# A two-layer transformer kernel: first norm by tile, two early norms by transfers, the last unit's exponentials next to its projections, the last tile by column halves

## The chip, the cores and the metric

The kernel runs on one core of a Trainium2 chip. Times are device microseconds of one launch. Three runs of the kernel before gave 637.04, 637.12 and 637.52; the median is 637.12. The profile is of one more execution, which took 638.02.

## The reference

Four sublayers, each wrapped the same way: `x = x + layernorm(f(layernorm(x)))`, on x of 2 batches x 512 rows x 256 columns, all in float32.

```python
x = x + _layernorm(_L0_attn_ref(_layernorm(x), ...))   # its own norm with gain and bias, q, k, v of 16 heads of 128,
                                                       # rope on q and k, causal softmax, out projection, residual
x = x + _layernorm(_L0_ffn_ref(_layernorm(x), ...))    # 256 -> 2048 gate and up (4-bit weights with block scales),
                                                       # gelu(gate) * up, 2048 -> 256
x = x + _layernorm(_L1_attn_ref(_layernorm(x), ...))   # linear attention, below
x = x + _layernorm(_L1_ffn_ref(_layernorm(x), ...))    # 256 -> 688 gate and up, weights lut[idx], silu(gate) * up, 688 -> 256

def _L1_attn_ref(x, W_qkv, W_out):
    q, k, v = jnp.split(x @ W_qkv.T, 3, axis=-1)       # 16 heads of 16
    q, k = phi(q), phi(k)                              # elu(x) + 1
    kv_cumsum = jnp.cumsum(k * v, axis=2)
    k_cumsum = jnp.cumsum(k, axis=2)
    out = q * kv_cumsum / (q * k_cumsum + EPS)
    return out @ W_out.T * HD ** (-0.5)
```

## The kernel before

The 1024 rows are 8 tiles of 128 rows; two tiles are a unit, so a batch has two units and there are four (u = 0 to 3). x stays on chip from its load to its last store.

**Order of the work.** Each engine runs its own list of instructions in order; the lists are written by hand. PE's list is the backbone: `slot(i)` for the 32 heads of both batches (scores of head i, the projections of q and k for head i+1, the out projection of head i-2, attention over values of head i-1), then `ffn_hidden` and `ffn_out` of the four units, then `silu_hidden` and `silu_out` of the four units. The work between the stages (norms, linear attention, stores) is written as generators, "chains", that yield when they would have to wait. `now` is a planner's clock of PE, `times` holds planned ends of all instructions, `until(tile)` is how long a tile still takes by that plan, and `poll()`, called between pieces of PE work, goes on with each chain that is due. So a chain's instructions stand in the engines' lists where the plan says that their inputs will be ready. Plan and chip may differ: then an engine waits.

**Loads.** `load(name, gg)` issues a weight group's transfer on SP's queue; a group serves two heads, and each weight has two buffers. At the start, SP and ACT issue the four tiles of batch 0 in turn, then ACT issues `cols_sb` (biases, gain and bias of the norm), SP the weights. `load("q", 2)` and `load("k", 2)` stand in slot 1 ahead of `turned_p(1)`. `turned_p(i)` turns the softmax of head i in 32x32 blocks on DVE and moves the blocks to their place by four transfers (pT; one buffer); head 0's are issued by SP and ACT, the others by SP.

**First norm** (`first_norms(0, 0.0)`). While x lands, PE runs 12 matmuls of the identity as warm-ups (`warm_up(WARM)`). DVE takes the statistics of the tiles (bn_stats, bn_aggr, then ve), POOL raises ve to -0.5 (rstd), DVE works out shift = -mean * rstd for tiles 0 and 1, and ACT applies n = x * rstd + shift; tiles 2 and 3 are centred and scaled on DVE. PE transposes n in order of tiles into two PSUM banks, with one more warm-up behind tile 0, and gain and bias are applied on the way out of PSUM: by ACT for the half of tiles 0 and 1, by DVE for that of 2 and 3. The first projection, of q for head 0, is done in the same two halves.

**Norms between the stages** (`norms(u, y, stage, to)`). The statistics of y (POOL works out ve, rstd and shift), a wait for all of them, then for each tile x += y * rstd on DVE and the statistics of the new x; then ACT writes the normed x to n, and n is transposed into `to`. Two ways of doing that: with `by_blocks`, two DVE transposes of 32x32 blocks and four SP transfers put it in place; otherwise four PE transposes into one PSUM bank and two ACT copies, each copy written behind the two transposes of its half. Before, `by_blocks` holds only when `late` has its pools, that is after attention, and never for the last norm (u = 3, stage 3). So the norms of units 0 and 1 of stage 1, which run beside the attention of batch 1, are transposed on PE.

**Linear attention** (`linear_attention(u)`). Projections of k, q and v (8 matmul records of 128x256 each on PE); ACT takes relu(-k), relu(k) and the same of q, with a yield after each; after v's projection ACT takes exp of the two negative parts, then DVE adds -1 and 1 and POOL adds the parts. Running sums on DVE (ks, kvs), the quotient (den), and the output projection into a bank with tag "o". `silu_out` and `ffn_out` use the banks of tag "o" too; each tag has two banks.

**End.** `silu_out(u)` gives for each of two tiles six matmuls (12 records) into a bank "o", and begins `written`: statistics, rstd and shift on POOL, x += y * rstd, x += shift on DVE, one SP transfer of 128 KB.

Of the kernel before, what the change touches and what calls it, by code (L numbers as in the profile page):

```python
# [32 lines left out]
HT = 2  # L33
# [7 lines left out]
NEG = -1e30  # L41
WARM = 12
REST = INTER - (NO - 1) * P
# [145 lines left out]
def sandwich_kernel(  # L189
# [96 lines left out]

    x0 = [const.tile([P, NT, D], F32, name=f"x0_{b}") for b in range(B)]
    for t in range(NT):
        (scalar if t % 2 else sync).dma_start(
            out=x0[0][:, t, :], in_=x[0][t * P : (t + 1) * P, :]  # L290
        )
    cols_sb = const.tile([P, 3 * NH + 2 * NK], F32, name="cols_sb")
    scalar.dma_start(out=cols_sb, in_=cols)
    cos_sb = const.tile([P, S], F32, name="cos_sb")
# [47 lines left out]
    def norms(u, y, stage, to, eps=EPS, strided=False):  # L342
# [4 lines left out]
        first = [stats(t, eps) for t in y]  # L347
        yield until(*(t for f in first for t in f))
        second = []
        for j in range(HT):  # L350
            add_scaled(x[j], y[j], first[j][0])
            second.append(stats(x[j], EPS))
# [3 lines left out]

        by_blocks = late and (u, stage) != (NUNIT - 1, 3)
        for j in range(HT):
# [24 lines left out]
        else:  # L383
            pt = bank("t")
            for kc in range(NK):
                for j in range(HT):
                    transpose(
                        pt[:, kc * TU + j * P : kc * TU + (j + 1) * P],
                        n[:, j, kc * P : (kc + 1) * P],
                    )  # L390
                scalar.copy(
                    to[:, :, kc].rearrange("p a j t -> p j a t"),
                    pt[:, kc * TU : (kc + 1) * TU].rearrange("p (j a t) -> p j a t", j=HT, a=4),
                )
# [103 lines left out]
    with ExitStack() as at:  # L498
# [54 lines left out]
        def first_norms(b, wait):  # L553
# [19 lines left out]
            def shifted(k, ts):  # L573
                vector.scalar_tensor_tensor(
                    shift[:, k, ts], mv[:, ts, 0], -1.0, rstd[:, k, ts], ALU.mult, ALU.mult
                )

            def norm(k, t, to):
                scalar.activation(
                    to,  # L580
                    x0[b][:, t, :],
                    AF.Identity,
                    bias=shift[:, k, t : t + 1],
                    scale=rstd[:, k, t : t + 1],
                )

            def finished(t):
                shifted(0, slice(t, t + 1))
                norm(0, t, n[t // HT][:, t % HT, :])
# [46 lines left out]
            else:  # L636


                statistics(0)
                variance(0)  # L640
                statistics(1)
                factor(0)
                variance(1)
                statistics(2)
                factor(1)
                variance(2)
                statistics(3)
                factor(2)
                variance(3)
                finished(0)  # L650
                factor(3)
                finished(1)
                centred(2)
# [8 lines left out]
                for j in range(2):  # L662
                    for kc in range(NK):
                        affine(
                            vector if j else scalar,
                            xT0[b][:, kc, j * TU : (j + 1) * TU],
                            halves[j][:, kc * TU : (kc + 1) * TU],
                            kc,
                        )
# [321 lines left out]
        def slot(i):  # L991
            b, h = divmod(i, NH)
            g2, odd = divmod(i, HG)
            if odd == 0:
                load("v", g2 + 2)
# [72 lines left out]
            if i == 0:  # L1068
                values(1, 0)
            elif i == 1:  # L1070
                load("q", 2)
                load("k", 2)
            if now_in:
# [47 lines left out]
    def linear_attention(u):  # L1121
# [18 lines left out]

        k, q, v, ek, eq = of("k"), of("q"), of("v"), of("ek"), of("eq")
        for part, e, f in ((1, ek, k), (0, eq, q)):
            ps = project(part, "mm")
            scalar.activation(flat(e), ps, AF.Relu, scale=-1.0)
            scalar.activation(flat(f), ps, AF.Relu)
            yield until(f)
        ps = project(2, "s")
        scalar.copy(flat(v), ps)

        for e, f in ((ek, k), (eq, q)):  # L1150
            scalar.activation(e, e, AF.Exp, scale=-1.0)
        yield until(ek, eq)
        for e, f in ((ek, k), (eq, q)):
            vector.tensor_scalar(e, e, -1.0, 1.0, ALU.add, ALU.add)
            pool.tensor_add(f, f, e)
        yield until(k, v)
# [10 lines left out]
        running_sum(ks, k)  # L1167
        yield until(ks, q)
        vector.tensor_mul(den, q, ks)
# [12 lines left out]
        yield until(lT)  # L1182
        po = bank("o")
        for t in range(HT):
# [59 lines left out]
    def silu_out(u):  # L1244
        for t in range(HT):
            po = bank("o")[:, :D]
            for o in range(NO):
                matmul(po, hT2[u % 2][:, o, t * P : (t + 1) * P], wd[:, o, :], o == 0, o == NO - 1)
                if o % 2 and o + 1 < NO:
                    yield  # L1250
            begin(written(u, t, po))
            yield

    def written(u, j, y):
        x = xs[u][:, j, :]
        rstd, shift = stats(y, EPS)
        yield until(rstd, shift)
        add_scaled(x, y, rstd)
        vector.tensor_scalar(x, x, shift, None, ALU.add)
        row = ((u % 2) * HT + j) * P  # L1260
        sync.dma_start(out=out[u // 2][row : row + P], in_=x)

# [105 lines left out]
```

## Time and profile before

| | |
|---|---|
| median of 3 runs | 637.12 us (637.04 to 637.52) |
| the profiled execution | 638.02 us, span of its instructions 636.2 us |
| busy share of the span | PE 98%, DVE 77%, ACT 47%, POOL 43% |
| granted TensorE clock | 0.999 |
| first projection starts | 8.18 us |
| heads 2 to 30, one slot each | 11.20 us in most |
| last matmul ends, x of the last tile is done | 630.8, 633.4 us |

Time is counted in us from the span's start. A row of the timeline has the start, the duration (of merged rows, from the first start to the last end), the engine, the line, the operation, the tile written and those read, the shapes and the number of instructions; in brackets is the idle time of the engine just before, and what ended it. Line 181 and line 272 are helpers that record every operation of DVE, ACT and POOL, and every matmul: the tiles tell which one it is. A float32 matmul has two records. PEld is PE's loading of weights; SPq and ACTq are rows of an instruction queue that issues transfers. Ends of matmuls are modelled, so consecutive rows of PE overlap by some 0.2 us, and PE's time is better counted from start to start.

### The profile page before, as it was taken

How to read it: one execution, taken by the hardware profiler on the slowest of the kernel's cores; microseconds unless marked ns; L12 is line 12 of the kernel's file. 1: busy time of each engine (PE TensorE's matmuls, PEld its weight loads, DVE VectorE, ACT ScalarE, POOL GpSimd, SP SyncE). 2: the span in 40 equal slices, each digit the busy share in tenths (PEclk: the TensorE clock that was granted, in tenths of full speed). 3: DMA queues.
4: the chain of work that ended last, by engine and by line, in shares of the span. 5: the costliest groups of instructions: out<-in, count | busy, mean ns of one | idle time of the engine just before them, and what ended most of it. 6: DMA issues, size and time to landing. Idle time of an engine off the chain costs nothing.

```text
span 636.2 us, 8205 instructions
## 1 busy us (share of the span) xinstructions
PE 622.6 (98%) x2506; PEld 463.1 (73%) x2506; DVE 487.8 (77%) x1152; ACT 299.6 (47%) x656; POOL 275.1 (43%) x350
## 2 busy tenths in 40 slices
PE   8999999999999999999999999999999999999896
PEld 6566666666666666665666688888888888888775
DVE  7869889877887989898988999769966651662852
ACT  3645666656655556666565651232233223333220
POOL 3354657445454465754767400450350350351441
PEclk9999999999999999999999999999999999999999
DMA  7456475564556547446352421311000000001010
GB/s 249 117 142 182 119 180 148 112 183 122 141 150 160 164 117 189 129 109 186 87 139 73 100 61 45 108 28 31 2 18 16 1 17 18 0 20 32 0 35 16
DMA packets 41276, 59.54 MB, mean 94 GB/s; under 512 B 4880, under 2 KB 28688, under 8 KB 41232
## 3 DMA queue, kind: packets, MB, share of 16 engines
q1 hardware_dynamic: 40512, 58.30, 34.8%
q10 hardware_dynamic: 720, 0.72, 0.5%
q8 instruction: 20, 0.33, 0.2%
q14 instruction: 24, 0.20, 0.1%
HBM read 28.33 MB, written 1.05 MB: 46 GB/s over the span
## 4 chain that ended last, share of the span: by engine, by line
PE 91%; DVE 4%; ACT 1%; DMA 1%; issue 1%; POOL 1%; ACTq 0%; POOLq 0%; DVEq 0%
PE ps_mm L272 37%; PE ps_s L272 20%; PE ps_o L272 20%; PE ps_t L272 13%; DMA pT<-turned 1%; PE ps_o L535 1%; DVE rr L181 1%; DVE den L181 1%; PE ps_t L278 0%; DVE x L181 0%; DVE st L181 0%; ACT L181 0%; DVE ra L181 0%; DVE ks L181 0%; POOL rstd L181 0%
## 5 line engine op out<-in xcount | busy, mean ns | idle before, releaser
L181 POOL TENSOR_TENSOR wg<-wg,scratch 128x752 f32<-128x752 f32 x30 | 53.5, 1784 | 98.7 <-DVE scratch L181 98.7
L181 DVE SCALAR_TENSOR_TENSOR rr<-ps_mm,cols_sb,sin_sb 64x512 f32<-64x512 f32 (+1 forms) x126 | 93.4, 741 | 2.6 <-ACT ra L181 0.2
L272 PE MATMUL ps_mm<-xT,wg 128*128 128x256 f32 (+1 forms) x352 | 85.4, 380 | 0.8 <-ACT si L181 0.7
L181 ACT ACTIVATE p<-p,mn 128x512 f32<-128x512 f32 (+3 forms) x128 | 70.6, 553 | 30.4 <-DVE mn L181 30.4
L272 PE MATMUL ps_s<-xT,wu 128*128 128x256 f32 x336 | 81.0, 379 | 0.0
L272 PE MATMUL ps_o<-wd,hT 128*128 128x256 f32 x352 | 78.2, 379 | 0.4 <-DVE x L181 0.4
L272 PE MATMUL ps_t<-pT,v 128*128 128x512 f32 (+3 forms) x256 | 74.3, 433 | 1.9 <-DMA pT<-turned 1.9
L272 PEld LDWEIGHTS ps_o<-wd,hT 128*128 128x128 f32 x352 | 66.8, 190 | 9.8 <-DVE x L181 0.8
L272 PEld LDWEIGHTS ps_mm<-xT,wg 128*128 128x128 f32 (+1 forms) x352 | 66.1, 189 | 10.7 <-ACT si L181 1.1
L181 DVE CUSTOM_DVE_ANT_0 p<-ps_s,mask 128x512 f32<-128x512 f32 (+2 forms) x96 | 46.0, 510 | 32.0 <-PE ps_s L272 31.6
L272 PEld LDWEIGHTS ps_s<-xT,wu 128*128 128x128 f32 x336 | 63.8, 190 | 8.7
L272 PEld LDWEIGHTS ps_t<-pT,v 128*128 128x128 f32 x256 | 48.6, 190 | 29.3 <-issue 15.3
L181 ACT ACTIVATE p<-p,rs 128x512 f32<-128x512 f32 (+3 forms) x128 | 61.4, 550 | 11.2 <-DVE rs L181 9.2
L272 PEld LDWEIGHTS ps_o<-wo,oT 128*128 128x128 f32 x256 | 48.6, 190 | 19.0 <-issue 13.6
L181 POOL TENSOR_TENSOR qT<-ra,rr 128x512 f32<-128x512 f32 x32 | 40.8, 1276 | 48.4 <-DVE rr L181 46.3
L272 PE MATMUL ps_s<-kT,qT 128*128 128x512 f32 (+2 forms) x192 | 60.8, 452 | 0.2 <-DVE kT L181 0.2
L272 PE MATMUL ps_o<-wo,oT 128*128 128x256 f32 x256 | 60.5, 379 | 0.0
L272 PE MATMUL ps_mm<-xT,wq 128*128 128x512 f32 (+1 forms) x128 | 58.4, 580 | 0.2 <-ACT xT L181 0.2
L272 PE MATMUL ps_mm<-xT,wk 128*128 128x512 f32 x124 | 58.3, 592 | 0.0
L181 DVE STREAM_TRANSPOSE turned<-p 128x512 f32<-128x512 f32 (+3 forms) x128 | 54.1, 481 | 2.1 <-DMA pT<-turned 1.0
L272 PEld LDWEIGHTS ps_s<-kT,qT 128*128 128x128 f32 x192 | 36.0, 190 | 26.8 <-issue 16.0
L272 PE MATMUL ps_mm<-wv,xTv 128*128 128x256 f32 x232 | 54.9, 379 | 0.0
(129 smaller groups left out, 917.0 us busy)
## 6 DMA issues: line engine op xcount, KB each, us to landing
pT<-turned SPq DMA_DIRECT2D x126, 208.0 KB, 3.8
wo<-in_wo SPq DMA_DIRECT2D x17, 256.0 KB, 4.0
wq<-in_wq SPq DMA_DIRECT2D x16, 256.0 KB, 3.9
wk<-in_wk SPq DMA_DIRECT2D x16, 256.0 KB, 4.0
wv<-in_wv SPq DMA_DIRECT2D x16, 256.0 KB, 4.1
xT<-tr SPq DMA_DIRECT2D x36, 64.0 KB, 2.2
pk_g<-in_gate_p SPq DMA_DIRECT2D x4, 256.0 KB, 5.2
sc_g<-in_gate_s SPq DMA_DIRECT2D x8, 128.0 KB, 4.4
```

The costliest lines, as they stand in the source:

```text
L181: return write(*args, **more)
L272: nc.tensor.matmul(out, lhsT=lhsT, rhs=rhs, start=start, stop=stop, **more)
L535: nc.tensor.matmul(warm[:, :P], lhsT=ident, rhs=ident, start=True, stop=True)
```

## The change

- First norm: `cols_sb` is loaded ahead of x; SP loads tiles 0 and 1, ACT tiles 2 and 3. Statistics, variance and factor are written tile by tile; the shift of tiles 0 and 1 is worked out on POOL; ACT applies gain and bias to all four quarters. There are 9 warm-ups instead of 12.
- The loads of q's and k's group 2 move from slot 1, ahead of `turned_p(1)`, to the start of slot 2, behind it.
- `norms` waits for each tile's rstd alone, and `by_blocks` holds for all norms but the last one. In the last one, both copies stand behind all four transposes.
- For the last unit, `linear_attention` writes exp, the DVE addition and POOL's addition right behind each projection, without the yields between; its output goes to a bank of tag "t".
- The last tile of `silu_out` is computed by two column halves of 128. Its `written` takes statistics by half, works out ve on DVE, centres y on DVE, adds it scaled to x in one step, and stores 64 rows each through SP and ACT.

```diff
-WARM = 12
+WARM = 9
...
+    cols_sb = const.tile([P, 3 * NH + 2 * NK], F32, name="cols_sb")
+    scalar.dma_start(out=cols_sb, in_=cols)
     for t in range(NT):
-        (scalar if t % 2 else sync).dma_start(
+        (scalar if t >= HT else sync).dma_start(
             out=x0[0][:, t, :], in_=x[0][t * P : (t + 1) * P, :]
         )
-    cols_sb = const.tile([P, 3 * NH + 2 * NK], F32, name="cols_sb")
-    scalar.dma_start(out=cols_sb, in_=cols)
...
         first = [stats(t, eps) for t in y]
-        yield until(*(t for f in first for t in f))
         second = []
         for j in range(HT):
+            yield until(first[j][0])
             add_scaled(x[j], y[j], first[j][0])
             second.append(stats(x[j], EPS))
...
-        by_blocks = late and (u, stage) != (NUNIT - 1, 3)
+        by_blocks = (u, stage) != (NUNIT - 1, 3)
...
+            for kc in range(NK):
                 scalar.copy(
                     to[:, :, kc].rearrange("p a j t -> p j a t"),
...
+            def shifted_row(t):
+                pool.tensor_scalar(
+                    shift[:, 0, t : t + 1], mv[:, t, 0:1], rstd[:, 0, t : t + 1], -1.0, ALU.mult, ALU.mult
+                )
...
-            def finished(t):
-                shifted(0, slice(t, t + 1))
+            def finished(t, engine=vector):
+                if engine is pool:
+                    shifted_row(t)
+                else:
+                    shifted(0, slice(t, t + 1))
                 norm(0, t, n[t // HT][:, t % HT, :])
...
-                statistics(0)
-                variance(0)
-                statistics(1)
-                factor(0)
-                variance(1)
-                statistics(2)
-                factor(1)
-                variance(2)
-                statistics(3)
-                factor(2)
-                variance(3)
-                finished(0)
-                factor(3)
-                finished(1)
+                for t in range(NT):
+                    statistics(t)
+                    variance(t)
+                    factor(t)
+                    if t < HT:
+                        finished(t, pool)
                 centred(2)
                 centred(3)
...
                         affine(
-                            vector if j else scalar,
+                            scalar,
...
         def slot(i):
             b, h = divmod(i, NH)
             g2, odd = divmod(i, HG)
+            if i == 2:
+                load("q", 2)
+                load("k", 2)
...
-            elif i == 1:
-                load("q", 2)
-                load("k", 2)
             if now_in:
                 turned_p(i)
...
+        last = u == NUNIT - 1
         for part, e, f in ((1, ek, k), (0, eq, q)):
             ps = project(part, "mm")
             scalar.activation(flat(e), ps, AF.Relu, scale=-1.0)
             scalar.activation(flat(f), ps, AF.Relu)
-            yield until(f)
+            if last:
+                scalar.activation(e, e, AF.Exp, scale=-1.0)
+                vector.tensor_scalar(e, e, -1.0, 1.0, ALU.add, ALU.add)
+                pool.tensor_add(f, f, e)
+            else:
+                yield until(f)
         ps = project(2, "s")
         scalar.copy(flat(v), ps)
...
         running_sum(ks, k)
-        yield until(ks, q)
+        if not last:
+            yield until(ks, q)
...
-        po = bank("o")
+        po = bank("t" if last else "o")
...
+            last = (u, t) == (NUNIT - 1, HT - 1)
+            for cs in [slice(0, P), slice(P, D)] if last else [slice(0, D)]:
+                for o in range(NO):
+                    matmul(
+                        po[:, cs],
+                        hT2[u % 2][:, o, t * P : (t + 1) * P],
+                        wd[:, o, cs],
+                        o == 0,
+                        o == NO - 1,
+                    )
...
+        st = small.tile([P, 2, 6], F32, tag="st", name="st_last")
+        mv = small.tile([P, 2], F32, tag="mv", name="mv_last")
+        for c in range(2):
+            vector.bn_stats(st[:, c, :], y[:, c * P : (c + 1) * P])
+        vector.bn_aggr(mv, st)
+        ve = small.tile([P, 1], F32, tag="ve", name="ve_last")
+        vector.tensor_scalar(ve, mv[:, 1:2], EPS, None, ALU.add)
+        rstd = small.tile([P, 1], F32, tag="rstd", name="rstd_last")
+        pool.tensor_tensor(rstd, ve, mhalf[:, :1], ALU.pow)
+        centred = acts.tile([P, HT, D], F32, tag="ln", name="centred")[:, 0, :]
+        vector.tensor_scalar(centred, y, mv[:, 0:1], None, ALU.subtract)
+        add_scaled(x, centred, rstd)
+        for engine, rows in ((sync, slice(0, P // 2)), (scalar, slice(P // 2, P))):
+            engine.dma_start(out=to[rows], in_=x[rows])
```

## The prediction

> **What bounds the kernel now.** I read the page first, then PE's waits, then the timelines around them.
>
> ```profile
> PE 622.6 (98%) x2506; PEld 463.1 (73%) x2506; DVE 487.8 (77%) x1152; ACT 299.6 (47%) x656; POOL 275.1 (43%) x350
> PE 91%; DVE 4%; ACT 1%; DMA 1%; issue 1%; POOL 1%; ACTq 0%; POOLq 0%; DVEq 0%
> ```
>
> The first line is busy time by engine, the second the chain that ended last, both of the page. PE's own waits (total, times, longest):
>
> ```profile
> PE ps_t L272 <- DMA pT<-turned: 1.9, 1, 1.9
> PE ps_o L272 <- DVE x L181: 1.5, 2, 1.1
> ```
>
> PE is the path: only what PE does not have to do, or its few waits, can shorten the span, plus the two ends where it has no work. The largest stand here, in its timeline (start, length; the bracket is the idle time before; two more, 0.36 at 611.44 and 0.82 at 294.14, are of the same kinds):
>
> ```profile
> 32.35 2.39 PE L272 MATMUL ps_t<-pT,v 128*128 128x512 f32 x8 [1.90 <-DMA pT<-turned]
> ...
> 255.70 2.32 PE L272 MATMUL ps_t<-pT,v 128*128 128x512 f32 x8
> 257.85 0.38 PE L278 MATMUL ps_t<-ident,ln 128*128 128x128 f32 x2
> 259.06 0.44 PE L278 MATMUL ps_t<-ident,ln 128*128 128x128 f32 x2 [0.82 <-ACT xT L181]
> 259.33 1.89 PE L272 MATMUL ps_mm<-wv,xTv 128*128 128x256 f32 x8
> ...
> 590.41 1.13 PE L272 MATMUL ps_mm<-xT,wg 128*128 128x256 f32 x4 [0.73 <-ACT si L181]
> ...
> 603.91 1.99 PE L272 MATMUL ps_o<-wout_sb,lT 128*128 128x256 f32 x8 [1.15 <-DVE x L181]
> ...
> 614.58 0.33 PE L278 MATMUL ps_t<-ident,ln 128*128 128x128 f32 x1 [0.17 <-ACT ln L181]
> 615.37 0.44 PE L278 MATMUL ps_t<-ident,ln 128*128 128x128 f32 x2 [0.46 <-ACT xT L181]
> ```
>
> Ends of matmuls are modelled, so I count by starts: a 128x256 record takes 0.216 us (8 in 1.73 from 259.33 to 261.06), a 128x128 one 0.11.
>
> **The first norm.** The first useful matmul (ps_mm<-xT,wq) starts at 8.18.
>
> ```profile
> 1.38 5.49 PE L535 MATMUL ps_o<-ident 128*128 128x128 f32 x24 [1.38 <-POOL ident masks.py:199]
> 6.66 0.43 PE L278 MATMUL ps_t<-ident,n 128*128 128x128 f32 x2
> ...
> 4.12 2.11 POOL L181 TENSOR_TENSOR rstd<-ve,mhalf 128x1 f32<-128x1 f32 x4 [2.32 <-DVE ve L181]
> 5.34 1.09 ACT L181 ACTIVATE n<-x,shift,rstd 128x256 f32<-128x256 f32 x2 [1.71 <-DVE shift L181]
> ```
>
> ACT has tile 0's n at 5.94, but its transposes stand behind 12 warm-ups until 6.66. With 9 (24 records in 5.28 by starts, so 0.44 a warm-up) they end at 5.4. New chain: statistics of tile 0 at 3.03 + 0.43, aggregate 0.18, ve 0.14 and gaps: rstd starts at 3.92 instead of 4.12. On POOL follow in order rstd 0 (0.55), shift 0 (0.27, as a later norm's at 629.94), rstd 1, shift 1, rstd 2, rstd 3, about 0.08 between: shift 1 at 5.8, rstd 3 at 6.9 (before: last rstd at 6.23). So ACT's second n ends at 6.4 as before, and DVE's centred tile 3 comes at 7.4 instead of 6.68. Transposes run in order, tile 3's last; q's first matmul then starts at about 7.65, 0.53 earlier, and its second half, with the affine now on ACT (4 x 0.51 from 6.8, ending 8.85 against DVE's 9.00), ends 0.65 earlier. ACT hides these two affines; DVE, idle from 6.7 to 8.0, loses nothing else. The queues keep their three ACT issues; cols_sb moving ahead of x costs x little (26 KB against 128 KB a tile) and may land tile 0 0.25 earlier, as it now shares the engines with less. Bounds without the clock: 0 (POOL's chain) to 0.9; I take **-0.65**, nearest the rows.
>
> Against it stands the clock. In the rows, warm-up records are 0.213 apart up to 6.45 and 0.11 apart from 6.8: half rate for 5.3 us of PE work. "TensorE: Matmul & The Clock Gate" of the Trainium skill, Part 1, says that the rate doubles after one busy window of about 3.4 us of a free-running clock, and Part 4 that transposes don't count as busy. By the rule, 12 warm-ups contain a whole window in (5.3 - 3.4)/3.4, 55% of phases, 9 (4.0 us) in 17%; else the first surely full window starts with the projections, and half rate until 11.1 to 14.5 costs half of 3.4 to 6.8 us, 1.7 to 3.4. The row would give -0.65, the rule up to +2.8. I take the row's: the 9 warm-ups, the one between transposes and the projections fill about three quarters of the window that opened at 3.3 here, and I doubt that a window must be wholly full. The range keeps the other end.
>
> **q2, k2 loads behind turned_p(1).** Before, SP issues wq and wk at 26.03 and 27.50, while head 0's pT (24.68 to 26.90 on SP and ACT) is in flight; ACT's two take a median 6.2 us to land against 3.8 on the page. Behind head 1's pT they no longer share its engines. PE is due at 28.56 + 1.73 = 30.29 and starts at 32.35: 2.06 lost. What is late next is kT of head 2: POOL ends it at 32.12 + 1.27 = 33.39, and its scores stand at 34.59, so 1.2 less a hop of 0.14 can be gained. **-1.05** (0.5 to 1.1). The price: SP now issues wq, wk at about 38, ahead of wv, wo and the pk_g load, which move back some 1.5 us each; pk_g has until ACT's cast at 46.47, and head 4's projection is at 48. Head 1's pT keeps its place ahead of them, head 2's (issued from 44.56) may land up to 1.5 later out of 2.3 spare. Hidden; without that cover some 0.5.
>
> **Two early norms by transfers** (units 0 and 1, stage 1). From 255.70 to 259.33 is 3.63, where a slot without a norm takes 2.16: 1.47 of PE each, twice **2.94** (four transposes and a wait for ACT's copy, at 257.85 and 292.94). New: two DVE transposes per norm (0.44 each in later norms), four SP issues of 0.6; ACT drops two copies of 0.37. SP waits for tr, but behind it stand loads, and the next pT, which comes later on DVE anyway; xT1 is needed 60 us later. DVE is what pays, since the slot also gets shorter:
>
> ```profile
> core 0: us, PE busy (x) PEld busy (x) DVE busy (x) ACT busy (x) POOL busy (x), PEclk, DMA share, GB/s
> 237.12:248.33 11.21, 11.21 (x42) 7.15 (x40) 10.97 (x27) 7.02 (x17) 8.63 (x10) 1.00 0.63 170
> 248.33:261.06 12.73, 11.91 (x46) 7.75 (x45) 11.67 (x32) 8.66 (x21) 7.08 (x7) 1.00 0.50 120
> 261.06:272.26 11.20, 11.20 (x41) 7.29 (x40) 9.21 (x21) 6.20 (x15) 6.62 (x7) 1.00 0.55 159
> ```
>
> 11.67 + 0.88 = 12.55 in a slot of 11.25: DVE falls 1.3 behind, and the next slot has 1.99 free. The second norm: 11.22 + 0.88 in 11.2, 0.9 behind, then 1.43 free. kT has only 0.4 to 0.8 to spare before PE's scores, so I charge 0.45 (0 to 2.2): **-2.5**.
>
> **The last unit.** ACT does k's and q's Exp at 587.30, after two yields; now they follow each projection. Three projections run in one piece, 576.57 to 581.75 (24 x 0.216), putting back silu_out(0)'s rest and hidden(1), which are not late. ACT: relus 578.49 to 579.58, table 1.28, Exp to 581.5, q's relus and Exp to 583.3, v 583.9, table again 585.2; the next si is due at about 586.3, so the 0.73 wait goes, and still two table loads. k is ready at 583.3 instead of 592.87; DVE and POOL then need 11.0 as before (592.91 to 603.91): lT at 595, xT3 by 607. PE has hidden(1), hidden(2), silu_out(1), silu_out(2) and wout until 613, so it does not wait for them. The "t" bank takes away the wait for written's x at 603.91 and at 611.44; all transposes ahead of the copies, and a cover of silu_out(2), the waits from 614.58. By starts from 588.65 to 616.81: 0.9, 1.3 and 0.5 at those three, 0.3 + 0.7 + 0.4 around the transposes, 0.3 of slow first records: 4.4. I leave 0.5 for transposes that still meet ACT: **-3.9** (2.5 to 4.4). The first[j][0] waits shorten chains that PE doesn't wait for: nothing; their cover is PE's backlog.
>
> **The last tile.**
>
> ```profile
> 631.56 0.22 POOL L181 TENSOR_SCALAR ve<-mv 128x1 f32<-128x1 f32 x1 [1.36 <-DVE mv L181]
> 633.06 0.35 DVE L181 TENSOR_SCALAR x<-x,shift 128x256 f32<-128x256 f32 x1
> ```
>
> Before, the chain is bn_stats at 630.82, aggregate, POOL's ve and pow, two DVE steps on x. From PE's end (630.79) to x is 2.62. New: second half's statistics about 0.30, aggregate 0.22, ve on DVE 0.17, pow 0.65, x 0.52, and 0.17 because DVE is in the first tile's x until PE ends: 2.03, so 0.6 less. Centring (0.45) hides under pow. 24 records of 0.112 instead of 12 of 0.216 cost PE 0.1; half a transfer on each of two queues, 0 to 0.2 less of 1.7. **-0.55** (0.2 to 0.8).
>
> **Sum** 0.65 + 1.05 + 2.5 + 3.9 + 0.55 = 8.65. The profiled execution took 638.02 (span 636.2, 1.8 around it), 0.9 above the median of 637.12; off the median: **628.5**.
>
> **Rivals.**
> - The clock slips one window at the start: 1.7 more, 630.2. For it the skill's rule, against it the nearly full window.
> - DVE becomes the bound of the norm slots and stays behind into the next ones: the full 2.2, perhaps more: 630.5 to 632. For it DVE's 10.97 of 11.21 in the slot before the first norm; against, the free slots after each.
> - The planner, whose times order the queues, sets the last unit's steps elsewhere and PE waits again: 3 of the 3.9 are not gained, 631.5.
> - Slower than before: PE stays at half rate. Each us of it costs 0.5: the gains are eaten when it lasts 17 us past 7.7, and from 20 us (27.7) on the kernel is over 0.2% slower; 30 us of it give 643.5. For it only the same page's note that the gate has been seen stuck for over 50 us; against, PE is busy from 8 on but for 2 us.
>
> **How the numbers follow.** A measurement here tells 0.2% (1.3 us) from no change. As computed 0.60 (626.8 to 629.8), clock slip 0.15, DVE 0.11, planner 0.07, slower or near nothing 0.07. Range 626.6 to 632.3: it leaves out the last case and the ends. Faster 0.92, same 0.03, slower 0.05.
>
> **What would show it.** Right: no L278 rows on ln at 250 to 300; ps_t<-pT first at about 30.6; no idle bracket over 0.3 on PE after 586; k's scan near 584; first wq matmul near 7.6 and 0.216 apart. Wrong: wq records 0.43 apart (clock); waits of PE on kT or on DVE p at 260 to 310; PE waits in 590 to 616; a POOL shift ending after 6.

## The result, and the profile after

Four runs of the changed kernel gave 631.17, 631.60, 632.86 and 633.01: median 632.23 us, against 637.32 (637.04 to 638.08) for the kernel before on the same chip. The ratio is 0.9917, with a 95% interval of 0.9897 to 0.9937. It is faster, by 5.1 us where 8.65 were predicted. The profiled execution took 631.60, its span is 629.8; before it was 636.2, so the two traces differ by 6.4.

The page's busy times and its chain that ended last:

```profile
PE 619.6 (98%) x2504; PEld 461.7 (73%) x2504; DVE 487.7 (77%) x1154; ACT 298.2 (47%) x654; POOL 277.8 (44%) x350
PE 95%; DMA 2%; DVE 1%; issue 0%; ACT 0%; POOL 0%; ACTq 0%; POOLq 0%
```

PE has 3.0 us less work (eight transposes and six warm-up records are gone, 12 records came with the halves of the last tile) and 95% of the chain instead of 91%. PE's waits (total, times, longest):

```profile
PE ps_t L272 <- DMA pT<-turned: 1.5, 1, 1.5
...
PE ps_t L278 <- DVE n L181: 1.3, 2, 0.9
PE ps_t L278 <- ACT ln L181: 0.4, 1, 0.4
```

The waits for x in the last stage, 1.5 before, are gone; a wait for `n`, in the first norm, is new. PE's timeline at the places that the prediction showed:

```profile
7.77 0.44 PE L278 MATMUL ps_t<-ident,n 128*128 128x128 f32 x2 [0.90 <-DVE n L181]
8.62 0.44 PE L278 MATMUL ps_t<-ident,n 128*128 128x128 f32 x2 [0.41 <-DVE n L181]
8.89 1.97 PE L272 MATMUL ps_mm<-xT,wq 128*128 128x256 f32 x8
...
16.13 1.96 PE L272 MATMUL ps_s<-kT,qT 128*128 128x512 f32 x6
...
32.54 2.39 PE L272 MATMUL ps_t<-pT,v 128*128 128x512 f32 x8 [1.49 <-DMA pT<-turned]
...
255.91 2.32 PE L272 MATMUL ps_t<-pT,v 128*128 128x512 f32 x8
258.07 1.89 PE L272 MATMUL ps_mm<-wv,xTv 128*128 128x256 f32 x8
...
304.61 1.89 PE L272 MATMUL ps_s<-kT,qT 128*128 128x512 f32 x6
...
594.55 1.89 PE L272 MATMUL ps_t<-wout_sb,lT 128*128 128x256 f32 x8
...
605.53 0.55 PE L278 MATMUL ps_t<-ident,ln 128*128 128x128 f32 x3 [0.35 <-ACT ln L181]
...
618.87 5.43 PE L272 MATMUL ps_o<-wd,hT 128*128 128x256 f32 x36
```

Read the rows as stretches between places that both traces have. In the trace of before, those that the prediction does not show are:

```profile
15.53 1.96 PE L272 MATMUL ps_s<-kT,qT 128*128 128x512 f32 x6 [0.17 <-DVE kT L181]
...
307.35 1.89 PE L272 MATMUL ps_s<-kT,qT 128*128 128x512 f32 x6
...
625.44 5.34 PE L272 MATMUL ps_o<-wd,hT 128*128 128x256 f32 x24
```

| stretch, to the start of | before | after | this stretch gave | predicted |
|---|---|---|---|---|
| scores of head 0 | 15.53 | 16.13 | +0.59 | -0.65 |
| values of head 0 (pT) | 32.36 | 32.54 | -0.41 | -1.05 |
| scores of head 26, past both norms | 307.35 | 304.61 | -2.92 | -2.5 |
| last `silu_out` | 625.44 | 618.87 | -3.83 | -3.9 |
| end of the span | 636.2 | 629.8 | +0.19 | -0.55 |

(The column "this stretch gave" is the change in how long the stretch lasts, by unrounded starts.) The two large steps came as worked out. The start and the end, worked out as gains, are losses in this pair of traces, and head 0's pT gives less than half.

Not all rows are equally firm. In this trace and those of the experiments below, the third stretch lasts 272.04 to 272.15 us in twelve of the thirteen traces that have the norms by transfers (the other, with a piece at half clock, 273.47), against 274.99 before. The fourth lasts 314.25 to 314.27 in all ten that keep the last unit as changed, against 318.09 and 318.12 in the two with the old one. The first two rows have no such firmness: the kernel with only the norms changed has the same code as the kernel before up to there, and its trace reached scores of head 0 at 15.24 instead of 15.53, and values of head 0 at 31.36 instead of 32.36.

Where the start goes is told by the timeline of DVE and ACT's queue:

```profile
1.17 0.93 ACTq L163 DMA_DIRECT2D x<-in_x  x2
...
5.18 0.15 DVE L181 TENSOR_SCALAR ve<-mv 128x1 f32<-128x1 f32 x1
6.56 0.43 DVE L181 BATCH_NORM_STATS2 st<-x 128x6 f32<-128x256 f32 x1 [1.22 <-DMA x<-in_x]
...
8.15 0.41 DVE L181 TENSOR_SCALAR n<-x,mv,rstd 128x256 f32<-128x256 f32 x1 [0.44 <-POOL rstd L181]
```

DVE waits 1.22 us for tile 3 of x and takes it at 6.56. It is now ACT's third issue, behind `cols_sb` and tile 2. In the trace of before:

```profile
1.64 0.45 ACTq L163 DMA_DIRECT2D cols_sb<-in_cols  x1
...
4.65 0.39 DVE L181 BATCH_NORM_STATS2 st<-x 128x6 f32<-128x256 f32 x1
```

There ACT's third issue was `cols_sb`, and it landed at 6.47, while DVE took tile 3 at 4.65 without a wait. So ACT's third place is the late one, whatever stands in it. What runs beside it is wq, which SP issues at 1.63, when ACT issues its third at 1.64: in the trace of before, and in the eight traces that have tile 3 in this place, ACT's third issue landed 0.17 to 0.28 us after wq, at 5.9 to 6.8.

The end is seen in the timeline of all engines and queues:

```profile
624.28 2.73 SPq L163 DMA_DIRECT2D out<-x  x2
...
625.94 0.48 DVE L181 SCALAR_TENSOR_TENSOR x<-centred,rstd_last,x 128x256 f32<-128x256 f32 x1 [0.16 <-POOL rstd_last L181]
626.45 0.59 ACTq L163 DMA_DIRECT2D out<-x  x1
```

(The row of SP merges the first tile's store and the first half of the last.) x is done 2.12 after PE's end, where 2.62 was measured before and 2.03 predicted. But SP's wait for the stores ends at 628.77, 2.35 after x; before, with one store of 128 rows, it ended 1.74 after x.

### The profile page after: what moved, and what is told of

It reads as the page before. It is cut to its first block, busy times and chain, and to the rows that moved or that the text cites. A ratio compares the mean times of both kernels' runs of the same rounds, so it can differ in the third digit from the quotient of the medians.

```text
span 629.8 us, 8201 instructions
## 1 busy us (share of the span) xinstructions
PE 619.6 (98%) x2504; PEld 461.7 (73%) x2504; DVE 487.7 (77%) x1154; ACT 298.2 (47%) x654; POOL 277.8 (44%) x350
## 3 DMA queue, kind: packets, MB, share of 16 engines
HBM read 28.33 MB, written 1.05 MB: 47 GB/s over the span
## 4 chain that ended last, share of the span: by engine, by line
PE 95%; DMA 2%; DVE 1%; issue 0%; ACT 0%; POOL 0%; ACTq 0%; POOLq 0%
PE ps_mm L272 38%; PE ps_o L272 22%; PE ps_s L272 21%; PE ps_t L272 14%; DMA pT<-turned 1%; DMA x<-in_x 1%; PE ps_t L278 0%; DVE turned L181 0%; DVE rr L181 0%; ACT ln L181 0%; POOL rstd L181 0%; ACTq L163 0%; DVE st L181 0%; DVE ra L181 0%; ACT p L181 0%
## 5 line engine op out<-in xcount | busy, mean ns | idle before, releaser
L272 PE MATMUL ps_o<-wd,hT 128*128 128x256 f32 (+1 forms) x364 | 78.2, 372 | 0.0
```

Of the source, the lines that this page charges most:

```text
L272: nc.tensor.matmul(out, lhsT=lhsT, rhs=rhs, start=start, stop=stop, **more)
```

## The experiments

Executions of one kernel differ by more than the changes of one part: a stretch of 3.413 us, in which TensorE's granted clock is half, comes in some and not in others. Half of it, 1.7, is the most that it can cost; by starts the traces below show 0.9 to 1.4 for one. So the trace is compared stretch by stretch, and each run's granted clock is named where it explains a time. The experiments ran on three more chips, where the kernel before took 638.53, 638.12 and 638.20; a ratio is taken to the kernel before on the same chip. Three parts were not run alone: the waits for each tile's rstd, the order of the last norm's transposes and copies, and the column halves of the last tile.

**Tile 3 on SP.** SP issues it ahead of wq; ACT keeps `cols_sb` and tile 2.

```diff
-        (scalar if t >= HT else sync).dma_start(
+        (scalar if t == HT else sync).dma_start(
```

> The changed kernel with x's tile 3 issued by SP instead of ACT, ahead of wq. In the changed kernel's trace it was ACT's third issue (1.64) and its statistics began at 6.56, 2.5 us after the third tile's, and q's first matmul at 8.89 against 8.18 before the change. Theory (the late tile alone makes the start slower, because it shares the engines with wq's and wk's larger packets): tile 3's statistics begin near 5.2 and q's first matmul at 7.5 to 7.7, 1.2 to 1.4 us earlier; the median falls by as much, to 630.8 to 631.0, or more if a shorter wait also keeps the clock from slipping. Rival (POOL's chain of rstd and shift is the limit): q's first matmul stays above 8.3 and the median within 0.5 of 632.2.

Measured: 630.55 (630.23 to 630.67), ratio 0.9873 (0.9856 to 0.9889), span 628.9. From its timelines of DVE and PE:

```profile
5.68 0.42 DVE L181 BATCH_NORM_STATS2 st<-x 128x6 f32<-128x256 f32 x1
...
6.72 0.76 PE L278 MATMUL ps_t<-ident,n 128*128 128x128 f32 x4 [0.50 <-ACT n L181]
7.64 0.44 PE L278 MATMUL ps_t<-ident,n 128*128 128x128 f32 x2 [0.16 <-DVE n L181]
7.91 1.97 PE L272 MATMUL ps_mm<-xT,wq 128*128 128x256 f32 x8
```

DVE no longer waits for tile 3. The first projection starts at 7.91 instead of 8.89, scores of head 0 at 15.16 instead of 16.13. One word in the order of loads is the cause of the lost start. It is not being third in a queue that is late: as SP's third issue, with wq behind it, the tile is there when DVE comes to it. The four runs lie within 0.44 of each other; those of the changed kernel are 1.84 apart. How much the start loses differs between executions: with tile 3 third on ACT, scores of head 0 start at 15.46 to 16.25 in the six traces without a stretch at half clock, with tile 3 on SP at 15.16 to 15.51 in three.

**Twelve warm-ups.** The changed kernel with the old number of them.

```diff
-WARM = 9
+WARM = 12
```

> The changed kernel with 12 warm-ups instead of 9, nothing else. Its runs fall in two groups, 631.2 and 631.6 at a granted clock of 0.998, and 632.9 and 633.0 at 0.996 to 0.997. Theory (the clock slips in about half of the runs, because 9 warm-ups leave part of a window of the clock's monitor idle): all runs lie in the faster group, median 631.2 to 631.8, clock 0.998 in each; the start costs nothing, as tile 3 makes PE wait until 8.6 anyway. Rival (the two groups are noise or come from elsewhere): both groups stay and the median is 632.2.

Measured: 631.79 (631.14 to 632.18), ratio 0.9892 (0.9875 to 0.9909), span 629.4. Scores of head 0 started at 15.46, but not because of the warm-ups: in this execution tile 3 landed near 5.9 instead of 6.5, and PE still waited 0.35 for its `n`. The clock was full from 6.45 on, as with 9 from 5.88. The clock does not fail to rise with 9: in the nine traces with 9 it rose between 4.32 and 7.57. Whether 12 keep it from falling again is not settled: no run of these four is as slow as 632.9 and 633.0, as the theory had it, but four runs against four do not show it.

**All of head 0's pT on SP.** A test of another reason for the pT wait: that ACT's queue is slow.

```diff
-                (scalar if i == 0 and j % 2 else sync).dma_start(
+                sync.dma_start(
```

> The changed kernel with all four transfers of head 0's pT on SP (two of them were on ACT). Attention of head 0 still waits: it starts at 32.54, 1.7 later than PE is free, though wq and wk of group 2 no longer run beside it. Theory (ACT's queue is what is slow: its two land 5.7 and 6.4 us after issue, while heads issued by SP alone have all four landed 6.5 us after the first issue): the last lands at about 31.8 instead of 32.4, and PE's wait falls by 0.6; median 0.6 lower. Rival (the engines' rate for these packets sets it, whichever queue): no change, or up to 0.8 later, since SP's four issues take 2.7 to 3.3 us in a row.

Measured: 632.47 (630.96 to 632.88), ratio 0.9897 (0.9879 to 0.9915). pT's last packet came 6.42 us after its last DVE transpose; in the changed kernel it was 6.32, and 6.47 for head 2, whose four are all SP's. ACT's queue is not what makes pT late: between 6 and 7 us is what these four transfers take in the ten traces without the loads beside them.

The profiled execution shows something else, which can explain the 1.8 us between the runs of the changed kernel:

```profile
7.99 0.44 PE L278 MATMUL ps_t<-ident,n 128*128 128x128 f32 x2 [1.15 <-DVE n L181]
8.84 0.44 PE L278 MATMUL ps_t<-ident,n 128*128 128x128 f32 x2 [0.41 <-DVE n L181]
9.12 3.41 PE L272 MATMUL ps_mm<-xT,wq 128*128 128x256 f32 x8
```

and by stretches (the PE column is its busy time; PEclk is the granted clock):

```profile
core 0: us, PE busy (x) PEld busy (x) DVE busy (x) ACT busy (x) POOL busy (x), PEclk, DMA share, GB/s
5.91:9.32 3.41, 1.80 (x11) 1.12 (x10) 1.50 (x5) 1.46 (x4) 0.95 (x2) 1.00 1.03 355
9.32:12.73 3.41, 3.41 (x9) 2.70 (x8) 1.62 (x4) 2.15 (x3) 1.58 (x2) 0.50 0.86 269
```

The clock had risen, at 5.91. In the window that followed, PE waited for tile 3 and was busy 1.80 of 3.41 us; the next window ran at half rate, eight wq records took 3.41 instead of 1.97, and scores of head 0 started at 17.69 instead of 16.13. From the first wq record to these scores it took 8.58 us instead of 7.23, so the half clock cost 1.35; the other 0.2 is a tile 3 that came later still. In the profile of the changed kernel the window 5.88 to 9.29 had PE busy 2.02, and the clock stayed. The late tile thus costs up to 1 us by its wait, and 1.35 more here, where the windows fell badly. The changed kernel's runs agree: 631.2 and 631.6 at a mean clock of 0.998, 632.9 and 633.0 at 0.997 and 0.996. This mean alone is not proof, since it also counts the half clock behind PE's last matmul: the trace with tile 3 on SP has 0.997, and no window lost while PE worked.

**The whole first norm as before**, with all other parts of the change.

```diff
-WARM = 9
+WARM = 12
...
-        (scalar if t >= HT else sync).dma_start(
+        (scalar if t % 2 else sync).dma_start(
...
-                for t in range(NT):
-                    statistics(t)
-                    variance(t)
-                    factor(t)
-                    if t < HT:
-                        finished(t, pool)
+                statistics(0)
...
+                finished(1)
...
-                            scalar,
+                            vector if j else scalar,
```

> The changed kernel with the first norm's whole part put back: 12 warm-ups, the x tiles by turns on SP and ACT ahead of the columns, statistics interleaved, shifts 0 and 1 after factors 2 and 3 on VectorE, the affines split between ACT and VectorE. Theory A (tile 3 as ACT's third issue makes PE wait 0.90 and 0.41 us and now and then drops the clock for a window): the first wq matmul starts at 8.2 instead of 8.89 and scores(0) at 15.5 instead of 16.13; no window at half rate after 9; the time is 0.6 below the changed kernel's 631.2 to 631.6, 630.6, and its runs lie within 1 us of each other. Rival B (the new first norm is worth its 0.65 as I had it, and the slip comes from elsewhere, such as the columns or the warm-ups): scores(0) stays at 16 or later and the time is 632 or more.

Measured: 630.30 (629.89 to 630.93), ratio 0.9878 (0.9863 to 0.9893), span 628.4; wq at 7.99, scores of head 0 at 15.34, no window at half rate. So the new first norm, as it was changed, is a loss here: 1.4 us by the spans. Of these, 0.79 lie ahead of the scores of head 0; 0.6 is pT, which PE took up 6.70 after the last transpose here and 7.30 after it in the changed kernel. Ten traces with the loads behind head 1's pT show anything from 6.6 to 7.5 for that, so only the 0.79 is put down to the norm.

**The q2 and k2 loads back in slot 1.**

```diff
-            if i == 2:
-                load("q", 2)
-                load("k", 2)
...
+            elif i == 1:
+                load("q", 2)
+                load("k", 2)
```

> The changed kernel with q's and k's group 2 loaded in slot 1 again, ahead of head 1's pT. In four kernels with the move, head 0's pT lands 6.3 to 6.9 us after its last DVE transpose, as any later head's does (6.5 for head 2); before the change it took 7.1. Theory (the move takes away a small contention only): 7.1 again, PE starts attention of head 0 0.2 to 0.8 later after its q started, median 0.4 higher. Rival (the loads were no contention at all, the difference is scatter): landing within the 6.3 to 6.9 and the median unchanged.

Measured: 635.96 over eight executions, ratio 0.9950 (0.9929 to 0.9971): 3.7 above the changed kernel's median (2.1 by the ratios; 3.3 above the kernel with the last output in a bank of tag "o", below, which ran on the same chip), though this step gave only 0.41 between the traces. The profiled execution was the odd one, at 630.97 with a clock of 0.998; two took 634.2 and 634.5 at 0.997 and 0.996, five 635.9 to 636.3 at 0.993 and 0.994. A second profile was taken of the same kernel:

> A second profile of the kernel with the q2 and k2 loads back in slot 1, whose profile showed 629.2 while seven other executions took 634.2 to 636.3. Theory A (the loads share the engines with pT of head 0, which then lands later, and PE's longer wait at attended(0) drops the clock for a window or two): PE's wait there is 3 to 5 us instead of 1.65, with records at half rate behind it, and the span is 632 to 634.5. Rival B (the loss is at the last unit or at the start, and the loads have no part in it): the wait at attended(0) is 1.5 to 1.9 and the missing 3 to 5 us lie elsewhere. If the span is 629 again, it stays open.

Measured: 634.57, span 632.8. Its PE timeline and its windows:

```profile
28.88 1.89 PE L272 MATMUL ps_t<-wv,xTv 128*128 128x256 f32 x8
34.11 3.81 PE L272 MATMUL ps_t<-pT,v 128*128 128x512 f32 x8 [3.34 <-DMA pT<-turned]
37.75 1.89 PE L272 MATMUL ps_s<-kT,qT 128*128 128x512 f32 x6
```

```profile
30.13:33.55 3.41, 0.63 (x3) 0.20 (x2) 1.50 (x2) 2.27 (x5) 3.33 (x3) 1.00 0.63 212
33.55:36.96 3.41, 2.85 (x4) 1.51 (x5) 1.69 (x4) 0.00 (x0) 0.14 (x1) 0.50 0.01 5
```

PE took pT up 9.14 us after the last transpose; the first profile of this kernel had 7.29, the kernel before 7.70, the one with only the norms changed 7.00, all four with the loads beside pT. Three of these four lie near the 6.6 to 7.5 of the traces without them, so it is the one execution that shows the delay. The last pT landed at 33.97 and the wq group of heads 4 and 5 at 34.17, so they were under way together. PE waited 3.34 instead of 1.5, was busy 0.63 us in that window, and ran the values of head 0 at half rate: 1.8 for the wait and 1.4 for the clock. The loads beside pT do what was predicted of them, but not in each execution, and then by more. That the loads make the runs slower is shown by the edit; that it goes by this wait rests on one profile. The runs 1.7 higher, at 0.993 and 0.994, would be those in which the start loses a window as well; that is inferred from clock and time, since none of them was profiled.

**The two early norms alone**: the kernel before with one line changed.

```diff
-        by_blocks = late and (u, stage) != (NUNIT - 1, 3)
+        by_blocks = (u, stage) != (NUNIT - 1, 3)
```

> The kernel before with one line of the change: by_blocks holds in all norms but the last, so the two early norms are turned by DVE and transfers. Theory (PE's 1.47 us in each is all gained, DVE's 0.9 us more in each hides in its idle time): 2.9 us less than before, ratio 0.9954, and PE's waits on kT or DVE p between 240 and 310 stay under 0.1. Rival (DVE pays, as the prediction charged): 2.0 to 2.5 less.

Measured: 634.69 over ten executions (634.2 to 637.2), ratio 0.9953 (0.9939 to 0.9967), which is 3.0 us; by the spans it is 3.8 (632.4), of which 1.0 had come by the values of head 0 (31.36), ahead of any norm. No record of PE starts over 0.09 late between 240 and 310. The remaining 2.8 is the step's, nearly all of its 2.94, and it stands by itself.

**The last unit's exponentials behind v again**, and the yields between, with the bank of tag "t" kept.

```diff
-        last = u == NUNIT - 1
+        last = False
...
-        po = bank("t" if last else "o")
+        po = bank("t" if u == NUNIT - 1 else "o")
```

> The changed kernel with the last unit's exponentials behind v's projection again, with the yields, but with the output still in a bank of tag t. Theory (the early exponentials are the larger part of the last stage's 3.8 us: they bring lT from 604 to 592 and take PE's wait for ACT's si away): PE waits again 0.7 to 0.9 for si near 583 and around the last norm's transposes, 1.5 to 2.5 us slower than the changed kernel. Rival (the bank alone did it, PE has enough other work either way): within 0.5.

Measured: 638.93 over 14 executions (636.46 to 641.06), ratio 1.0007 (0.9994 to 1.0019): as slow as the kernel before, and 6.6 behind the changed kernel from the values of head 0 to the end of the span. I had expected a third of that. Its PE timeline:

```profile
604.34 5.34 PE L272 MATMUL ps_o<-wd,hT 128*128 128x256 f32 x24
612.79 0.48 PE L278 MATMUL ps_t<-ident,ln 128*128 128x128 f32 x1 [3.11 <-ACT ln L181]
614.12 0.90 PE L278 MATMUL ps_t<-ident,ln 128*128 128x128 f32 x3 [0.85 <-ACT ln L181]
615.48 2.07 PE L272 MATMUL ps_mm<-xT,wg 128*128 128x256 f32 x4 [0.46 <-ACT xT L181]
617.35 1.71 PE L272 MATMUL ps_s<-xT,wu 128*128 128x256 f32 x4
```

With the bank of its own, PE no longer waits for x at `wout`; it runs ahead to all work that does not hang on the last norm, and then stands 3.11 us before the norm's transposes. That gap empties a window, and the clock is half from 611.90 to 618.72: eight records of wg and wu take 3.41 from 615.48 to 618.89 instead of 1.73. Of the 6.6, 4.1 is these waits (4.4 less the 0.35 left in the changed kernel); the rest is mostly the clock, 1.7 in these eight records alone. This unit's stretch lasts 320.9 here and 318.1 before, so without the early exponentials the other edits of this unit do harm. What the early exponentials give is mostly this: the chain of the last unit ends while PE still has other work.

**The last output in a bank of tag "o".**

```diff
-        po = bank("t" if last else "o")
+        po = bank("o")
```

> The changed kernel with the last unit's output projection in a bank of tag o again. Theory (both o banks hold silu_out(1)'s tiles when the projection comes, and it holds one while silu_out(2) wants two): PE waits 1.0 to 1.5 for written's x ahead of wout and up to 0.5 ahead of silu_out(2)'s second tile, 1.3 to 1.8 slower than the changed kernel. Rival (with the chain 9 us earlier the banks are free by then): within 0.3.

Measured: 632.61 (631.02 to 634.21), ratio 0.9910 (0.9891 to 0.9929), span 630.9. Of two waits for written's x in the kernel before, one is back and is shorter:

```profile
595.52 1.99 PE L272 MATMUL ps_o<-wout_sb,lT 128*128 128x256 f32 x8 [0.51 <-DVE x L181]
```

By starts it costs 0.67, and the next record comes 0.10 late. At `silu_out(2)` nothing waits. So the bank is worth 0.8 (the spans differ by 1.1, of which 0.3 had come by the values of head 0), less than I had expected: the earlier chain alone has taken away the rest. The run times do not tell 0.8 from nothing (ratios of 0.9910 and 0.9917); the stretch does, with 315.03 against 314.26.

**One store.** The last tile goes out as 128 rows through SP.

```diff
-        for engine, rows in ((sync, slice(0, P // 2)), (scalar, slice(P // 2, P))):
-            engine.dma_start(out=to[rows], in_=x[rows])
+        sync.dma_start(out=to, in_=x)
```

> The changed kernel with the last tile stored by one SP transfer of 128 rows instead of two of 64 rows by SP and ACT. In the changed kernel's trace the two were issued in 0.57 and 0.59 us (a whole tile's took 0.33 before) and SP's wait for them ended 2.32 after the issue (1.69 before). Theory (two queues that issue at once slow each other, and the half packets land no earlier): the issue takes 0.33 again, the end comes 0.6 us earlier, median 631.6. Rival (the landing is late for another reason, such as the store of the tile before): no change, within 0.2.

Measured: 630.72 (630.28 to 632.26), ratio 0.9884 (0.9865 to 0.9904), span 628.8. From x to the end of SP's wait it takes 1.74, as before the change; with two halves 2.35. This repeats: 1.74 to 1.75 in all five traces with one store, 2.34 to 2.36 in all nine with two. Its issue takes 0.332 us; two at once, on SP and ACT, take 0.567 and 0.590. Its row of SP has the same two stores' issues:

```profile
623.87 2.50 SPq L163 DMA_DIRECT2D out<-x  x2
```

where 2.73 stood above (0.23 for the slower issue; the landing is later by the rest of the 0.60). So 0.60 of the 1.0 by which the spans differ is the store; 0.37 had come by the values of head 0, where tile 3 was a little earlier in this execution. Two halves on one queue were not tried, so it is open how much is due to the halves and how much to the second queue.

**Both repairs**: tile 3 on SP and one store, with 9 warm-ups (the first expectation) and with 11 (the second).

```diff
-        (scalar if t >= HT else sync).dma_start(
+        (scalar if t == HT else sync).dma_start(
...
-        for engine, rows in ((sync, slice(0, P // 2)), (scalar, slice(P // 2, P))):
-            engine.dma_start(out=to[rows], in_=x[rows])
+        sync.dma_start(out=to, in_=x)
```

> The changed kernel with tile 3 issued by SP ahead of the wq load, and the last tile stored by one issue of SP. Theory A (two independent losses: 0.96 us in the start of scores(0), 0.6 in the last store): the span is 628.3, which is 628.9 of the kernel with tile 3 on SP less 0.6; the time is 629.9, ratio about 0.986. Rival B (the store's 0.6 is within what runs differ by, because the end of the program waits for something else too): 630.5, ratio 0.9873, no different from tile 3 on SP alone.

> The same as the last, with 11 warm-ups instead of 9 (two more of 0.43 us, which end near 6.24 instead of 5.38). Theory A (with tile 3 early, 9 warm-ups already hand over to the first norm's transposes in time for the clock): the same time within 0.3 us, 629.9. Rival B (the first transposes of the norm run behind the longer warm-up): scores(0) 0.3 to 0.5 later, 630.3. Rival C (9 warm-ups still leave the clock at half in some executions): best11's runs lie within 0.6 us of each other and those of 9 warm-ups are 1.5 us apart.

Measured: 629.93 (629.53 to 630.23) with 9, 629.82 (629.72 to 630.06) with 11; both ratios 0.9871 (0.9856 to 0.9886 and 0.9854 to 0.9888), below the interval of the changed kernel. The spans are 627.7 and 627.9. Values of head 0 start at 31.10 and 31.19, and PE no longer waits 0.9 for `n`; two rows of the one with 11:

```profile
8.16 2.06 PE L272 MATMUL ps_mm<-xT,wq 128*128 128x256 f32 x8 [0.17 <-ACT xT L181]
...
15.51 1.96 PE L272 MATMUL ps_s<-kT,qT 128*128 128x512 f32 x6
```

With 9, scores of head 0 start at 15.25. They differ by no more than the runs do. The time and the span are those of theory A, but the ratio is no better than with tile 3 on SP alone (0.9871 and 0.9873, on two chips); what the store gives stands on the traces, where the stretch behind the last `silu_out` lasts 10.34 in all three kernels with one store of the new tile and 10.94 or 10.95 in the nine with two. The fastest version found keeps the norms by transfers, the loads behind head 1's pT, the last unit and the last tile's halves. A gain of the new first norm, even when repaired, is not shown: scores of head 0 start at 15.16 to 15.51 in its three traces, and at 15.24 to 15.53 in the three with the old one.

## Why the prediction was right or wrong

Direction and order of the large parts were right: norms and last unit, 6.4 of the 8.65, gave 6.75. The median came 3.7 above the predicted time. It misses the times worked out as most likely, 626.8 to 629.8, and lies 0.07 inside the stated range. That range had been left wide for rivals of which two did not come and one came in another place, so that the median is still inside is luck. Of the 3.7, 2.25 stands between the traces (8.65 less 6.4); the rest is that the profiled execution was 0.9 above its median before, and 0.6 below it after.

- **First norm (-0.65, became +0.59 in this trace).** The chain was right piece by piece: POOL's shift 1 ended at 5.74 (5.8 predicted), ACT's second n at 6.37 (6.4), warm-ups at 5.38 (5.4). The step that failed is "the queues keep their three ACT issues; cols_sb moving ahead of x costs x little". I weighed its bytes and not its place in the queue, where it pushes tile 3 beside wq. The trace of before had the number, 6.47 for ACT's third landing, and DVE had taken tile 3 at 4.65 there. Centred tile 3 came at 8.56, against the 7.4 that I put down. Tile 0 did not land earlier either (3.00 against 3.01).
- **The clock.** The prediction took the rows' side against the page "TensorE: Matmul & The Clock Gate" of the Trainium skill, Part 1, as I read it, that a window must be wholly busy. The rows' side held: with the exponentials back, PE began at 1.38 and the clock rose at 4.32, behind a window that was 86% full, and in the changed kernel it rose at 5.88. That transposes do not count as busy, the prediction's other premise, does not fit the kernel with both repairs and 9 warm-ups: there a window with 2.77 us of warm-ups did not raise the clock, and the next did, with 2.07 us of other work and the rest of it transposes. The rival was put at the wrong door. It comes not as a clock that fails to rise, but as one that falls again because PE waits for tile 3. It cost 1.35 and 0.9 in the two traces that have it at the start (all of pT on SP, and the exponentials back), where 1.7 was given; by time and clock two of the changed kernel's four runs had it.
- **q2 and k2 loads (-1.05, -0.41 between the traces, 2.1 to 3.7 in the runs with the loads put back).** The place was right, and the price was hidden as said: head 2's pT has 2.16 to spare, 2.31 before. The term failed in two ways. I compared 6.2 us to landing with 3.8 of other heads on the page; counted from the last transpose to the last packet, head 0 took 7.10 before and head 2 took 6.31, so in that execution there was 0.8 to gain at most. And one execution does not show a wait's spread: from the last transpose to PE the same loads gave 7.0 in one profile and 9.14 in another, and a wait that empties most of a window also halves the clock. Why most runs of the kernel before were spared stays open: on the chip of this experiment six of its 25 took 639.4 or more, the others 638.8 at most, and none of the six was profiled.
- **Early norms (-2.5, became -2.92).** The 0.45 charged for DVE was not paid. The stretch of the first norm, and the next:

```profile
248.51:259.80 11.29, 11.29 (x42) 7.38 (x42) 10.49 (x30) 7.70 (x19) 5.56 (x4) 1.00 0.48 122
259.80:271.00 11.20, 11.20 (x42) 7.28 (x40) 10.35 (x26) 6.20 (x15) 6.28 (x6) 1.00 0.72 184
```

  DVE, the third number pair after the stretch, has 10.49 and 10.35 where I had added 0.88 to 11.67 and left 9.21. Pieces have moved into the next slot, which had room: the last aggregates of the following norm's statistics, which stood at 259.02 and 259.55 before, come at 270.05 and 270.57. My sum held them where they had stood. So the rival of a bound DVE did not come.
- **Last unit (-3.9, became -3.83).** Right in size, and in what was left: 0.35 at one transpose. Its parts were not independent: without the early exponentials the other edits of this unit lose 2.8, since their waits gather in one.
- **Last tile (-0.55, became +0.19).** The chain to x was right (0.50 of 0.6), and so was PE's 0.1. The step that failed is "half a transfer on each of two queues, 0 to 0.2 less of 1.7": it is 0.6 more.
- Neither the planner nor a clock stuck at half came.

## What to carry to other kernels

When loads are reordered, look up when the n-th issue of each queue landed before and what was issued beside it, and give the late place to what is needed last: the bytes of the load moved ahead say little. A wait of PE is priced by its length and by the window that it empties; several profiles, or the spread of the runs beside their mean clock, can tell whether a wait of 1.5 us is 3 in another execution. Splitting the last store over two queues is worth a trial of its own before it is counted as a gain.

## What the runs showed that was not expected

- The clock falls after one window of 3.413 us in which PE was too idle. In windows without transposes it fell after 1.20 us of work and less, and held after 1.48 (both repairs and 11 warm-ups, at 621.55), 1.69 (the kernel before, at 30.63) and more. In windows of the first norm, which hold transposes, it fell after 1.80 and 1.91 and held after 2.02 and more. Matmul ends are modelled, so each is good to some 0.2; that the two kinds of window have different bounds rests on two falls.
- It rises after a window that is 86% full of warm-ups, which run at half rate themselves (2.94 us, exponentials back), and did not after 81 and 80% (2.77 us with both repairs and 9 warm-ups, 2.72 with the last output in a bank of tag "o").
- Two stores of 64 KB, issued at once from two queues, end 0.60 us later after x than one of 128 KB: 2.35 against 1.74, within 0.02 in all fourteen traces.
- Among the kernels with q's and k's loads behind head 1's pT, runs differ by 1.0 to 4.6 us where tile 3 is late, and by 0.3 to 1.0 where it is early. With the loads beside pT they differ by 2.2 us or more on the three chips of the experiments, whatever the first norm. In these runs, removing a wait at the front of the kernel narrowed the measurement as well as lowering it.
